# Sends of two per step and two pairs begun per period in a two-layer graph-attention and expert kernel

## Chip, cores and metric

The kernel runs on one core of one Trainium2 chip. The metric is the device time of one execution in microseconds (us), lower is better; the time before is the median of three runs. An engine is named as the profile names it: PE is TensorE's matrix multiply and PEld its weight load, DVE is VectorE, ACT is ScalarE, POOL is GpSimd, SP is SyncE, which issues most of the transfers.

## What is computed

There are 64 graphs ("batches") of 256 nodes with 256 features, and one adjacency matrix. Two layers follow each other. `_layernorm` has no weights.

```
x = x + _L0_gnn_ref(_layernorm(x), adj, L0_gnn_W, L0_gnn_a)      # attention with 4 heads, elu
x = x + _L0_ffn_ref(_layernorm(x), L0_ffn_weight, L0_ffn_bias)   # one linear map
x = x + _L1_gnn_ref(_layernorm(x), adj, L1_gnn_W, L1_gnn_a)      # attention with 1 head, relu
x = x + _L1_ffn_ref(_layernorm(x), L1_ffn_router_w, w1, b1, w2, b2)

# _L1_ffn_ref: 8 experts, each token goes to its best two
logits = tokens @ router_w.T
rw, re = top_k(softmax(logits), 2);  rw = rw / rw.sum(-1)
for e in range(8):
    h = gelu(tokens @ w1[e] + b1[e])
    out = out + combine[:, e:e+1] * (h @ w2[e] + b2[e])          # out starts as tokens
```

The input of the last part is the normed `x`, and it is also added once to the result together with `x`.

## The kernel before

**Tiles.** A batch is two tiles of 128 rows. The first three parts and the router's logits of a batch are done by `batch_layers` (L485). The last part is not computed for all experts: 62 of the 64 batches are routed, that is, every row is written ("sent") to its two experts' regions in an HBM buffer `xs`, and the experts then work through full regions in units of 256 rows, called pairs of tiles. The last two batches are not routed; for them all eight experts are computed densely (`dense_expert`).

**Chunks.** Routed batches are grouped into chunks of 4 (twelve times), 2 (six times) and 1 (twice). A chunk of four batches has 8 tiles. When the logits of a chunk's last batch are there, `route` (L907) does, spread over several steps: the two best experts of every row (`top_two`), the place of every row in its expert's region (the matmuls L924 and L925 and the scan L933), the weights, the sends, and the allotting of pairs (`allot`, in two parts). A send is one indirect DMA issued by POOL (L890): 128 rows of one tile go to the places of their first or second expert, so a tile has two sends and a full chunk sixteen.

**Pairs.** In all there are 131 pairs: 1 for the first chunk, 8 for each of the other full chunks, 4 or 2 for the small ones, and 14 at the end that are not full. `expert_pair` (L710) loads a pair's rows (`xr`, L726, behind all the sends of its chunk), then its expert's weights (`we`), turns the rows on DVE (L116), computes the hidden layer on PE (`hidden`, L784, 8 matmuls) and gelu on ACT, the second product on PE (L799, 8 matmuls), adds the bias on DVE (L809) and multiplies by the row weights on ACT (L777). Then `scatter` (L814) adds the 256 rows into the output by two indirect DMAs with an add, issued by POOL (L820). The same row may be added to by two pairs, so the two DMAs of each pair wait until the two of the pair before have landed: the scatters form one chain.

**The order.** The program order of every engine is written by the loop at the end (L1058). Jobs are generators, and each `yield` ends a job's work in a step and gives its rank in the next one. A batch begins every third step (`TICKS = 3`), so three steps are one period, and the phase is the step's number modulo 3. Batches overlap: in one period, PE runs some part of each of several batches. In this document period n lasts from the first projection matmul (L384) of batch n to that of batch n+1.

- `later(rank, *phases)` lets a job sleep until a step of one of these phases (as long as batches are still beginning).
- Pairs begin in phase 1: each period adds to `credit`, and every credit of 1 begins one waiting pair. From `DRAIN_AT` (step 180) on the credit of a period is 3. From `QUIET` (step 209) on, one pair begins in every step.
- One scatter at most is begun in each step, behind the sends of that step.
- A pair that begins in step s is turned in s+2, goes through L784 in s+4, L799 in s+5 and L777 in s+6, and is scattered from s+7 on.
- The last dense batch is stored (L863) only after all scatters have landed.

Of buffers the steps of the prediction touch: 8 tiles `xng` of rows to be sent, 5 `xr`, 7 `we`, 9 `y` (the results that wait for their scatter).

Of the kernel before, what the change touches and what calls it, by code (L numbers as in the profile page):

```python
# [27 lines left out]
def kernel(  # L28
# [50 lines left out]
    def bank(name, shape):  # L79
        t = psum.tile([P, 2 * D], F32, tag="bank", name=name, bufs=8)  # L80
        n = 1
        for s in shape:
            n *= s
        t = t[:, :n]
        if len(shape) == 2:
            t = t.rearrange("p (a b) -> p a b", a=shape[0])
        elif len(shape) == 3:
            t = t.rearrange("p (a b c) -> p a b c", a=shape[0], b=shape[1])
        return t
# [317 lines left out]
    for i in range(2):  # L407
        t = keep.tile([P, NT, D + 1], F32, tag=f"q1_{i}", name=f"q1_{i}")
# [207 lines left out]
    def chunk_tile(shape, name, c, bufs=2, dt=F32):  # L616
        return keep.tile([P] + shape, dt, tag=name, name=f"{name}_{c}", bufs=bufs)
# [27 lines left out]
    def two_weights(less, second, ed):  # L645

        nc.vector.tensor_scalar(less, ed, 1.0, None, op0=ALU.add)
        nc.vector.reciprocal(less, less)
        nc.vector.tensor_tensor(second, ed, less, ALU.mult)
        nc.vector.tensor_tensor(less, less, second, ALU.subtract)  # L650
# [231 lines left out]
    def begin(job, rank):  # L882
        active.append([rank, len(order), job])
        order.append(job)
# [16 lines left out]
    def later(rank, *phases):  # L901

        yield rank
        while more and order_steps[-1] % TICKS not in phases:
            yield rank

    def route(c, row0, nt, n, last, xng, lg):  # L907

        rt = lambda shape, name, bufs=2, dt=F32: chunk_tile(shape, name, c, bufs, dt)
        vec, tt = nc.vector, nc.vector.tensor_tensor  # L910
        yield -90

        tail = rt([nt, 3], "tail")
        ohs, ed = top_two(c, nt, lg, tail[:, :, 0])
        m = rt([E, nt], "m")
        tt(m.rearrange("p e t -> p t e"), ohs[:, 0], ohs[:, 1], ALU.add)


        spread = nt == NTC
        yield from later(90, *((0,) if spread else (1, 2)))  # L920

        mf = m.rearrange("p e t -> p (e t)")
        pp = bank("pp", [2, E, nt])
        nc.tensor.matmul(pp[:, 0].rearrange("p e t -> p (e t)"), tri, mf, start=True, stop=True)  # L924
        nc.tensor.matmul(pp[:, 1].rearrange("p e t -> p (e t)"), ones, mf, start=True, stop=True)  # L925
        both = rt([2, E, nt], "both")
        vec.tensor_copy(both, pp)
        pre, tot = both[:, 0], both[:, 1]
        nc.scalar.activation(ed, ed, AF.Exp)
        tt(tot[:, :, 0], tot[:, :, 0], rows[0], ALU.add)  # L930
        run = rt([E, nt], "run")
        if nt == NTC:
            vec.tensor_tensor_scan(  # L933
                run.rearrange("p e t -> p (e t)"), scan_mask.rearrange("p e t -> p (e t)"),
                tot.rearrange("p e t -> p (e t)"), 0.0, ALU.mult, ALU.add,
            )
        else:
            for e in range(E):
                vec.tensor_tensor_scan(
                    run[:, e, :], ones[:, :nt], tot[:, e, :], 0.0, ALU.mult, ALU.add  # L940
                )
        rows[0] = run[:, :, nt - 1]
        tt(pre, pre, run, ALU.add)
        if spread:
            yield from later(90, 2)
        tt(
            ohs, ohs, pre.rearrange("p e t -> p t e")[:, None].to_broadcast([P, 2, nt, E]),
            ALU.mult,
        )
        posf = rt([2, nt], "posf")  # L950
        vec.tensor_reduce(posf, ohs, AX.X, ALU.add)
        pos = rt([2, nt], "pos", 4, I32)
        vec.tensor_copy(pos, posf)
        yield from later(90, *((0,) if spread else (1, 2)))
        two_weights(tail[:, :, 1], tail[:, :, 2], ed)
        for i, xe in enumerate(xng):
            vec.tensor_copy(xe[:, :, D + 1 :], tail[:, i * NT : (i + 1) * NT, :])
        parts = allot(c, n, False)
        if n and not spread:
            next(parts)  # L960
            ids, ef = next(parts)
        if last:
            ends_at = rt([E], "ends_at", 2, I32)
            vec.tensor_copy(ends_at, rows[0])
        yield from later(95, 1, 2)
        mark = len(sent)
        for t in range(nt):
            for k in range(2):
                send(xng[t // NT][:, t % NT, :], pos[:, k, t : t + 1])
            if n and spread and t in (1, 3):  # L970
                ids, ef = next(parts) or (None, None)
            if not last:
                yield from later(95, 1, 2)
            elif t % 2:
                yield 95
        needs = sent[mark:]
        if n:
            regs = {}
            waiting.extend(
                lambda j=j: expert_pair(j, n, ids, ef, regs, needs) for j in range(n)  # L980
            )
        if last:
            parts = allot(c + 1, FLUSH, True)
            next(parts)
            ids2, ef2 = next(parts)
            _, ends_sp = nc.values_load_multi_w_load_instructions(
                ends_at[0:1, :], engines=[mybir.EngineType.SP], min_val=0,
                max_val=(E * CAP - 1) * PAIR, skip_runtime_bounds_check_because="rows of a region",
            )
            filled = []  # L990
            for e in range(E):
                d = nc.sync.dma_start(
                    out=xs_d[bass.ds(ends_sp[e], PAIR), :].rearrange("(p t) c -> p t c", t=2),
                    in_=fill,
                )
                tc.declare_no_dep(
                    d.ins, query=SYNC, group="rows", reason="filling rows lie behind an expert's last row"
                )
                tc.add_to_no_dep_group("rows", d.ins)
                filled.append(d.ins.name)  # L1000
                nc.sync.nop()
            yield 95
            regs2 = {}
            waiting.extend(
                lambda j=j: expert_pair(j, FLUSH, ids2, ef2, regs2, filled)
                for j in range(FLUSH)
            )
# [45 lines left out]
    step, more, credit = 2, True, 0.0  # L1053


    DRAIN_AT, QUIET = TICKS * (B - 4), TICKS * B + 17
    SETUP_AT = 3
    with tc.manual_schedule():  # L1058
        while more or active or waiting or dense_jobs or scatters:
            phase = step % TICKS  # L1060
            if phase == 2 and more:
                nxt = next(batches, None)
                more = nxt is not None
                if more:
                    begin(nxt, 25)
            if step >= SETUP_AT and setup:
                begin(setup.pop(0)(), 90)
            if step >= QUIET:
                if waiting and len(scatters) < 3:
                    begin(waiting.pop(0)(), 90)  # L1070
            elif phase == 1:
                credit = min(credit + (2.0 if step < DRAIN_AT else 3.0), 3.0)
                while waiting and credit >= 1.0:
                    credit -= 1.0
                    begin(waiting.pop(0)(), 90)
            if dense_jobs and step % DENSE == 0:
                begin(dense_jobs.pop(0)(), 90)
            if scatters:
                def one():
                    scatter()  # L1080
                    return
                    yield
                begin(one(), 97)
            order_steps.append(step)
            queue = [(a[0], a[1], a) for a in active]
            heapq.heapify(queue)
            while queue:
                *_, entry = heapq.heappop(queue)
                entry[0] = next(entry[2], None)
                if entry[0] is not None and entry[0] < 0:  # L1090
                    entry[0] = -entry[0]
                    heapq.heappush(queue, (entry[0], entry[1], entry))
            if half_done:
                finish_norms(NT)
            active[:] = [a for a in active if a[0] is not None]
            step += 1
# [35 lines left out]
```

## Time and profile before

| | |
|---|---|
| median of three runs | 1650.05 us (1646.56 to 1652.72) |
| profiled execution, its own time | 1651.53 us |
| its span, first to last instruction | 1649.6 us |
| mean granted TensorE clock | 0.955 |
| PE busy | 1476.3 us, 89% of the span |
| DVE busy | 1323.8 us, 80% |
| ACT busy | 831.0 us, 50% |
| POOL busy | 889.4 us, 54% |
| scatters, L820 on POOL | 262, 1.585 us each |
| sends, L890 on POOL | 248, 1.012 us each |
| moved by DMA | 207.37 MB, mean 126 GB/s |

Busy times are sums over one execution, taken by the hardware profiler. The span is cut into stages that differ: about 300 us in which batches run and no pair does, some 900 us of steady periods with eight pairs to four periods, a stretch with three pairs in each period, and the end, in which no batch is left and pairs and scatters run out. A share of the whole span says little about what limits any one of these stages.

### The profile page before, as it was taken

How to read it: one execution, taken by the hardware profiler on the slowest of the kernel's cores; microseconds unless marked ns; L12 is line 12 of the kernel's file. 1: busy time of each engine (PE TensorE's matmuls, PEld its weight loads, DVE VectorE, ACT ScalarE, POOL GpSimd, SP SyncE). 2: the span in 40 equal slices, each digit the busy share in tenths (PEclk: the TensorE clock that was granted, in tenths of full speed). 3: DMA queues.
4: the chain of work that ended last, by engine and by line, in shares of the span. 5: the costliest groups of instructions: out<-in, count | busy, mean ns of one | idle time of the engine just before them, and what ended most of it. 6: DMA issues, size and time to landing. Idle time of an engine off the chain costs nothing.

```text
span 1649.6 us, 30216 instructions
## 1 busy us (share of the span) xinstructions
PE 1476.3 (89%) x8474; PEld 1299.8 (79%) x8474; DVE 1323.8 (80%) x4494; ACT 831.0 (50%) x1832; POOL 889.4 (54%) x853
## 2 busy tenths in 40 slices
PE   5898888999999999999999999999989997599930
PEld 4777777778888888888888888887878886488820
DVE  6888989999898989898989898999988877545510
ACT  0244344445666666565656666655555565343310
POOL 0121343444757575756575757566664677544444
PEclk8999999999999999999999999999999998799965
DMA  4812123254756565656666675756575667887633
GB/s 109 231 44 58 55 71 101 72 140 113 158 132 135 135 146 135 140 138 145 140 127 156 117 170 108 163 117 146 135 140 124 136 127 152 188 178 135 128 38 45
DMA packets 364132, 207.37 MB, mean 126 GB/s; under 512 B 264248, under 2 KB 334912, under 8 KB 363968
## 3 DMA queue, kind: packets, MB, share of 16 engines
q1 hardware_dynamic: 313344, 137.07, 33.7%
q0 software_dynamic: 49632, 67.39, 22.8%
q8 instruction: 70, 1.15, 0.3%
q10 hardware_dynamic: 992, 0.99, 0.2%
q14 instruction: 94, 0.77, 0.2%
HBM read 116.19 MB, written 89.15 MB: 124 GB/s over the span
## 4 chain that ended last, share of the span: by engine, by line
PE 62%; DVE 21%; DMA 5%; POOL 4%; issue 3%; ACT 3%; SPq 1%; DVEq 0%; POOLq 0%; ACTq 0%
PE pv L475 14%; PE ph L784 13%; PE py L799 12%; PE pq L384 5%; PE pq L419 5%; PE pf L529 4%; DVE z L461 3%; PE pt L368 3%; DVE stats L353 3%; DMA out_dram<-y,xt 3%; POOL out_dram L820 2%; PE pl L599 2%; DVE mv L354 2%; ACT xT L374 1%; PE pd L454 1%
## 5 line engine op out<-in xcount | busy, mean ns | idle before, releaser
L820 POOL DMA_INDIRECT out_dram<-y,xt x262 | 415.4, 1585 | 241.1 <-DMA out_dram<-y,xt 87.6
L475 PE MATMUL pv<-q,z 128*128 128x65 f32 (+1 forms) x2560 | 368.5, 299 | 3.7 <-DVE z L461 3.7
L475 PEld LDWEIGHTS pv<-q,z 128*128 128x128 f32 x2560 | 331.5, 194 | 15.5 <-DVE z L461 4.0
L361 POOL TENSOR_SCALAR rstd<-mv 128x4 f32<-128x4 f32 (+1 forms) x132 | 71.0, 538 | 432.2 <-DVE mv L354 337.1
L890 POOL DMA_INDIRECT xs<-xng,pos x248 | 250.9, 1012 | 68.8 <-issue 65.7
L799 PE MATMUL py<-w2s,hT 128*128 (+1 forms) x1176 | 266.1, 379 | 1.3 <-ACT hT L790 1.2
L784 PE MATMUL ph<-sT,we 128*128 128x256 f32 x1048 | 242.8, 385 | 11.8 <-DVE y L809 9.6
L799 PEld LDWEIGHTS py<-w2s,hT 128*128 128x128 f32 x1176 | 219.5, 190 | 30.0 <-ACT hT L790 2.2
L374 ACT COPY xT<-pt 128x512 f32<-128x512 f32 x192 | 113.3, 590 | 232.5 <-PE pt L368 232.4
L784 PEld LDWEIGHTS ph<-sT,we 128*128 128x128 f32 x1048 | 198.9, 194 | 38.5 <-issue 9.9
L461 DVE SCALAR_TENSOR_TENSOR z<-pd,q,mask 128x256 f32<-128x256 f32 x512 | 211.1, 473 | 0.3 <-PE pd L454 0.2
L790 ACT ACTIVATE hT<-ph,we 128x256 f32<-128x256 f32 x294 | 122.5, 472 | 126.2 <-PE ph L784 103.8
L362 POOL TENSOR_TENSOR rstd<-rstd,mhalf 128x4 f32<-128x4 f32 (+1 forms) x132 | 163.0, 1235 | 11.0
L777 ACT ACTIVATE y<-y,w 128x256 f32<-128x256 f32 x262 | 112.6, 501 | 100.1 <-DVE y L809 100.1
L353 DVE BATCH_NORM_STATS2 stats<-x 128x6 f32<-128x256 f32 x384 | 156.3, 407 | 2.2
L384 PE MATMUL pq<-wx,xT 128*128 128x268 f32 x512 | 139.2, 418 | 8.6 <-DVE wt L257 4.2
L419 PE MATMUL pq<-wx,xT 128*128 128x259 f32 x512 | 129.1, 394 | 15.6 <-ACT xT L374 15.6
L809 DVE TENSOR_TENSOR y<-py,b2s 128x512 f32<-128x512 f32 x131 | 85.8, 686 | 68.6 <-PE py L799 48.8
L384 PEld LDWEIGHTS pq<-wx,xT 128*128 128x128 f32 x512 | 101.8, 204 | 30.4 <-issue 6.9
L419 PEld LDWEIGHTS pq<-wx,xT 128*128 128x128 f32 x512 | 91.9, 189 | 42.0 <-ACT xT L374 30.7
L529 PE MATMUL pf<-wfT,xT 128*128 128x256 f32 x512 | 124.1, 386 | 0.0
L551 ACT ACTIVATE rel<-pv,rinv 128x256 f32<-128x256 f32 x128 | 53.9, 474 | 110.6 <-DVE rinv L482 110.5
(152 smaller groups left out, 2256.1 us busy)
## 6 DMA issues: line engine op xcount, KB each, us to landing
we<-wpack SPq DMA_DIRECT2D x139, 288.0 KB
xr<-xs SPq DMA_DIRECT2D x524, 64.0 KB
xblk<-in_x_dram SPq DMA_DIRECT2D x256, 64.0 KB
xin<-in_x_dram SPq DMA_DIRECT2D x64, 256.0 KB
out_dram<-base SPq DMA_DIRECT2D x64, 256.0 KB
out_dram<-y,xt POOLq DMA_INDIRECT x262, 3.9
xs<-xng,pos POOLq DMA_INDIRECT x248, 2.9
xs<-fill SPq DMA_DIRECT2D x9, 260.0 KB
```

The source lines that it names most:

```text
L353: nc.vector.bn_stats(stats[:, t, :], src[:, t, :])
L362: nc.gpsimd.tensor_tensor(rstd[:, :n], rstd[:, :n], mhalf[:, :n], ALU.pow)
L374: nc.scalar.copy(dst, pt)
L384: nc.tensor.matmul(pq.rearrange("p h c -> p (h c)"), xT[:, k, t * P : (t + 1) * P], wx[:, k, :], start=(k == 0), stop=(k == KT - 1),)
L419: nc.tensor.matmul(pq, xT[:, k, t * P : (t + 1) * P], wx1[:, k, :], start=(k == 0), stop=(k == KT - 1),)
L461: nc.vector.scalar_tensor_tensor(z[:, j, :], pd[:, i, :], q[:, j, h, d + 2 : d + 3], mask[:, j, :], op0=ALU.max, op1=ALU.mult,)
L475: nc.tensor.matmul(pv[:, h, :], z[:, j, t * P : (t + 1) * P], q[:, j, h, : d + 1], start=(j == 0), stop=(j == NT - 1),)
L529: nc.tensor.matmul(pf[:, t, :], xT[:, k, t * P : (t + 1) * P], wfT[:, k, :], start=(k == 0), stop=(k == KT - 1),)
L784: nc.tensor.matmul(ph[:, f, :], we[:, k * D + f * P : k * D + (f + 1) * P], xT[:, k, :], start=(k == 0), stop=(k == KT - 1),)
L799: nc.tensor.matmul(py[:, t, :], hT[:, f, t * P : (t + 1) * P], w2s[:, e, f * D : (f + 1) * D].rearrange("p e c -> p (e c)"), start=(f == 0 ...
L820: d = nc.gpsimd.indirect_dma_start(out=out_rows, out_offset=bass.IndirectOffsetOnAxis(ap=xt[:, t, 0:1].bitcast(I32), axis=0), in_=y[:, t, ...
L890: d = nc.gpsimd.indirect_dma_start(out=xs_d[: E * CAP * PAIR, :], out_offset=bass.IndirectOffsetOnAxis(ap=at, axis=0), in_=xe, in_offset=None,
```

## The change

Three lines of the schedule change. A chunk's sends no longer wait for phases 1 and 2: the first tile is sent in the step after the weights, and each further tile in the next step, whichever its phase. The second part of `allot` moves from behind tile 3 to behind tile 4. And the credit of a period in the steady part is capped at 2, where before a period without waiting pairs could leave a credit over, so that the next one began three.

```diff
@@ route
-        yield from later(95, 1, 2)
+        yield 95
         mark = len(sent)
         for t in range(nt):
             for k in range(2):
                 send(xng[t // NT][:, t % NT, :], pos[:, k, t : t + 1])
-            if n and spread and t in (1, 3):
+            if n and spread and t in (1, 4):
                 ids, ef = next(parts) or (None, None)
             if not last:
-                yield from later(95, 1, 2)
+                yield 95
             elif t % 2:
                 yield 95
         needs = sent[mark:]
@@ the loop that writes the order
             elif phase == 1:
-                credit = min(credit + (2.0 if step < DRAIN_AT else 3.0), 3.0)
+                credit = min(credit + 3.0, 2.0 if step < DRAIN_AT else 3.0)
                 while waiting and credit >= 1.0:
                     credit -= 1.0
                     begin(waiting.pop(0)(), 90)
```

## The prediction, made before the changed kernel was run

> **What bounds the kernel now.** I read the page's table of 40 slices first, then busy time by period (stretches cut at the first L384 of each batch), then the timelines of PE and POOL where a period was too long, and the end of POOL's timeline.
>
> ```profile
> PE   5898888999999999999999999999989997599930
> DVE  6888989999898989898989898999988877545510
> PEclk8999999999999999999999999999999998799965
> ```
>
> PE is full from slice 7 to the 33rd or so; before that it has room, and the last two slices have hardly any PE work. The periods, with the columns length, PE, PEld, DVE, ACT, POOL busy, clock, DMA share, GB/s:
>
> ```profile
> 315.40:333.70 18.30, 15.44 (x94) 12.56 (x95) 16.22 (x56) 7.22 (x18) 10.70 (x12) 1.00 0.36 87
> 333.70:351.20 17.50, 16.29 (x94) 13.89 (x94) 15.75 (x57) 7.34 (x18) 7.41 (x10) 0.90 0.43 99
> 437.20:462.40 25.20, 24.96 (x148) 22.31 (x146) 23.50 (x80) 17.76 (x41) 18.42 (x18) 1.00 0.76 171
> 462.40:483.80 21.40, 21.16 (x129) 18.94 (x129) 20.02 (x61) 12.76 (x28) 10.15 (x11) 1.00 0.49 121
> 483.80:505.10 21.30, 21.06 (x127) 18.85 (x126) 19.40 (x71) 12.95 (x29) 13.88 (x14) 1.00 0.57 115
> 505.10:523.60 18.50, 17.88 (x112) 15.79 (x111) 13.68 (x43) 8.43 (x18) 13.09 (x13) 1.00 0.77 150
> 1106.10:1125.50 19.40, 18.19 (x115) 16.18 (x114) 17.92 (x68) 8.67 (x19) 14.40 (x15) 1.00 0.79 159
> 1125.50:1156.80 31.30, 28.50 (x143) 25.09 (x142) 28.13 (x109) 18.35 (x40) 17.87 (x18) 0.89 0.54 132
> 1199.90:1221.70 21.80, 18.52 (x116) 16.30 (x115) 18.14 (x68) 9.87 (x21) 16.48 (x16) 1.00 0.81 172
> 1221.70:1251.60 29.90, 28.52 (x144) 24.87 (x143) 26.59 (x99) 18.32 (x40) 17.79 (x17) 0.89 0.62 126
> ```
>
> The first two rows (periods 18 and 19) have no pair. The next four are one cycle of a full chunk, periods 24 to 27, with 3, 2, 2 and 1 pairs: PE covers all but 0.3 us of the first three, so a pair is paid at its PE time, 25.2 - 21.4 = 3.8 us. (In most cycles the fourth takes 17.9, with PE at 17.6.) The last four rows are periods 55, 56, 59 and 60, with 1, 3, 1 and 3 pairs: there two chunks' routing overlaps, DVE is busy 28.1 us in period 56, and PE waits for it and then loses its clock:
>
> ```profile
> 1127.54 1.00 PE L475 MATMUL pv<-q,z 128*128 128x65 f32 x8
> 1131.11 5.17 PE L475 MATMUL pv<-q,z 128*128 128x65 f32 x24 [2.56 <-DVE z L461]
> ```
>
> The end is another matter. PE's last work ends at 1580.9, and this goes on until 1645:
>
> ```profile
> 1626.89 1.54 POOL L820 DMA_INDIRECT out_dram<-y,xt  x1 [2.98 <-DMA out_dram<-y,xt]
> 1628.74 1.54 POOL L820 DMA_INDIRECT out_dram<-y,xt  x1 [0.30 <-issue]
> 1633.21 1.54 POOL L820 DMA_INDIRECT out_dram<-y,xt  x1 [2.93 <-DMA out_dram<-y,xt]
> ...
> 1645.39 0.39 SPq L863 DMA_DIRECT2D out_dram<-base  x1
> ```
>
> Each pair's first scatter waits for the DMA before it. Alone, ten pairs from 1581.90 to 1639.68 take 57.78 / 9 = 6.42 us each; beside the last PE work, 16 from 1458.29 to 1575.57 take 7.33 each. The chain of scatters, not PE, ends the kernel, and by then it lags the products by 40 to 50 us.
>
> **The Trainium skill.** "DMA: Bandwidth & Descriptors", section "Anatomy of one DMA — SWDGE (gpsimd) path", puts most of a DMA's fixed 2 us on the confirmation that the data landed; here the second scatter is issued in 1.54 us and the next pair starts 4.5 us after its start, so the wait is of that kind. Its "Rules for kernel authors" say that an accumulating DMA must wait for an earlier one to the same bytes: the chain can't be shortened by issuing faster, only by leaving fewer pairs to its end. "TensorE: Matmul & The Clock Gate", "Part 1: The HAM clock gate", has the PE clock halved after an idle window of about 3.4 us; the trace agrees roughly: the clock stands at 0.5 for 6.8 us from 1132.4, after that wait (shorter, 2.56 us), and again from 1228.0. "PSUM — Partial Sum Buffer", "Engine vs sequencer instructions", calls GpSimd's queue strict FIFO: a send delays whatever stands behind it on POOL.
>
> **The change, part by part.** Counted in the written order of the two programs. Before, a full chunk sends two tiles per period: first send in step s, last in s+10, pairs begin in s+15. After: last send in s+7, pairs begin in s+9. So pairs begin two periods earlier, and each of the forty steady periods from 20 to 59 has two instead of 3, 2, 2, 1. Four pairs more are done by period 59. In steps 201 to 203, after the last batch has begun, two pairs pass L784 instead of 3. When batches end (step 209), 17 pairs wait instead of 20, and the program has 235 steps instead of 238. No instruction is added or removed but for registers.
>
> (a) The early pairs. Period 14 gets the first chunk's one pair and goes from 16.4 to the 17.9 of a one-pair period: +1.5. Period 16 loses it, but period 12, with the same routing and no pair, took 21.0 against its 21.2: -0.2. Periods 18 and 19 get two each and become 21.4: +3.1 and +3.9. Sum +8.2.
>
> (b) Even periods. 25.18 + 21.39 + 21.33 + 17.87 = 85.8 becomes 4 x 21.36 = 85.4: -0.33, in nine cycles -3. It needs DVE to keep up in the heavy period, which is also where `top_two` stands: DVE falls there from 23.5 by one pair's 1.75 us (0.69 turn, 0.69 L809, 0.37 weights) to 21.8, against PE's 21.1. Cover: L924 starts 3.0 to 3.9 us after its DVE operand is ready in periods 20 to 52; one L799 group less takes 1.8 of that. And the one-pair period ahead had left DVE late (the first L475 group of period 24 starts 0.4 us after its last z; after two-pair periods 4.3 to 5.5), which now goes. I take no stall; 0.9 us a cycle as the bad end, +9.
>
> (c) Periods 55/56 and 59/60. Against clean periods of the same pairs (17.87 + 25.18 = 43.05) they take 50.7 and 51.7, an excess of 7.7 and 8.7. With two pairs in 55 and in 59, PE gives DVE 3.5 us more ahead of the jam, the 2.56 us wait and the clock loss after it should shrink; the routing's DVE work stays. I take half, -8; ends 0 and -16.
>
> (d) Steps 201 to 203: one pair less at 3.65 of PE, in a stretch where other waits begin (PE stands 9.33 us in front of L924 at 1394.9); -2, ends 0 and -3.7.
>
> (e) The end. Three pairs fewer in the serial chain at 7.33: -22. Ends: 3 x 6.42 = 19, or 4 x 7.33 = 29 if the chain is full already where it is four ahead.
>
> (f) Sends. A send costs POOL 1.0 + 0.3 us, so two in phase 0 put 2.6 us ahead of the next rstd (L361, L362) in the send periods. POOL idled 1.2 to 9.4 us there waiting for DVE; hidden. Between the other rstd's the queue holds four sends and a scatter pair as before. If the cover were gone, `by` (L560) would be late by up to 2.6, with 1.4 to 7.6 us between its product `xng` and the PE transposes. Zero.
>
> (g) Loads behind sends. Steady chunks' first load is issued 28.4 us after the last send ends (1081.0 to 1109.5). Three steps of 7.1 us go: 7.1 left, against a landing of 2.9 (median) to 5.4. SP just clears it. Were it to wait, the input loads for batches two and three ahead queue behind, which have periods to spare, and `xr` itself is wanted two steps (14 us) later. Zero.
>
> The second part of `allot` stays in the same step (tile 3 before, tile 4 after). Sum: 8.2 - 3 - 8 - 2 - 22 = -26.8; 1651.5 - 26.8 = 1624.7 against the profiled execution's own time, which lies 1.5 above the median of the runs: 1623 there.
>
> **Rivals.** *Back to the start*: early pairs cost 10, nothing is relieved in (c) and (d), and the end gives 19: 1651.5 + 10 - 3 - 19 = 1639; with small stalls of half a microsecond per cycle, 1645. For it: DVE is as busy in 56 as PE. Against: that jam follows a one-pair period.
>
> *DVE becomes the bound of the routing period* (slower than before): period 24 and its like stay at 25.2 with two pairs because DVE's 21.8 and the latency of `top_two` fill it, while the light one still grows to 21.4. That is +3.5 in each of ten cycles, without (b) and (c): 1651.5 + 8.2 + 35 - 2 - 22 = 1671. For it: period 12, with routing and no pair, took 21.0 with DVE at 18.9 and L924 waiting 3.3 us for DVE. Against: the 3 us of slack above. It decides from about 2.7 us a cycle, if (c) fails too.
>
> *More than thought*: (c) goes wholly and the chain is four pairs shorter: 1651.5 + 8 - 3 - 16 - 4 - 29 = 1608.
>
> That the change does not do what it says is excluded: the written order shows 16 L784 matmuls in each period.
>
> **Numbers.** Forecast 0.72 (1612 to 1636), more 0.08, back to the start 0.11, slower 0.09. A change of 0.5% (8 us, below 1641.8 or above 1658.3) is what a measurement here can tell. Forecast, more and a little of the third give 0.82 faster; 0.1 the same, 0.08 slower. Range 1608 to 1643, from the larger gain to the middle of the second rival.
>
> **What would show it.** (b): periods 20 to 54 all 21.3 to 21.5 with PE at 21.1; wrong if a period with L924 reads 22 or more. (a): periods 18 and 19 at about 21.4. (c): the wait in front of L475 near period 56 and the half clock after it smaller or gone. (e): fewer scatters after PE's end or the same lag with an earlier end; wrong if scatters' spacing grows. (f), (g): waits of L726 for `xs` and of ACT for rstd no longer than now (32.3 and 83.4 us in all). The forecast fails as a whole if L924 waits for DVE in every chunk.

## Result, and the profile after

| | before | after |
|---|---|---|
| median | 1649.59 us of 4 runs (1646.56 to 1652.72) | 1633.01 us of 4 runs (1630.33 to 1633.96) |
| profiled execution, its own time | 1651.53 us | 1633.96 us |
| its span | 1649.6 us | 1632.2 us |
| mean granted TensorE clock | 0.955 | 0.958 |
| PE busy | 1476.3 us | 1476.4 us |
| DVE busy | 1323.8 us | 1322.6 us |

The changed kernel takes 0.9897 of the time before, with a 95% interval of 0.9875 to 0.9919. It is faster by about 17 us. PE and DVE do the same work as before. This is PE's row of the slices on the page of after, in tenths:

```profile
PE   5898989899999999999999999999999999589960
```

The stretch in which PE is below nine tenths now ends about a slice later, and the last slices hold a little more PE work than before. The slices are too coarse for a change of 1%, so I cut both traces at the first L384 of some batches, and at the last end of PE. The first cut is at period 5. Where the number of pairs is equal in both kernels, the row says so.

| stretch | before | after | difference |
|---|---|---|---|
| start to period 5 (no pairs) | 87.9 | 88.9 | +1.0 |
| periods 5 to 19 (1 pair before, 5 after) | 263.4 | 277.3 | +13.9 |
| periods 20 to 23 (8 pairs in both) | 86.0 | 85.8 | -0.2 |
| periods 24 to 55 (64 in both) | 688.3 | 686.6 | -1.7 |
| periods 56 to 59 (8 in both) | 96.2 | 96.2 | 0.0 |
| periods 60 to 62 (9 in both) | 79.9 | 76.0 | -3.9 |
| period 63 to PE's last end (41 pairs before, 37 after) | 279.4 | 267.9 | -11.5 |
| PE's last end to the end of the span | 68.7 | 53.6 | -15.1 |

The sum is -17.5, which is the -17.4 of the spans but for rounding. The early stretch pays, the end earns, and the long steady stretch between them stays as it was.

**The early stretch.** Here are periods 14 to 19 as one window, first of before and then of after. The columns are length; busy time of PE, PEld, DVE, ACT and POOL with the number of instructions; PE clock, DMA share and GB/s.

```profile
244.20:351.20 107.00, 96.05 (x584) 82.12 (x584) 98.12 (x338) 48.09 (x115) 47.70 (x57) 0.97 0.32 86
```

```profile
245.30:366.20 120.90, 109.68 (x648) 95.45 (x649) 108.52 (x374) 61.95 (x142) 53.03 (x61) 0.96 0.38 100
```

Four pairs more cost 13.63 us of PE. The time in which PE is idle was 10.95 us (107.00 - 96.05) and is 11.22 us now: taken together nothing of it was used, and the stretch grew by about the pairs' PE time. DVE is busy for about nine tenths of it in both. Its busy time grew by 10.4 us (108.52 - 98.12) and its idle time by 3.5, so the pairs cost more than the DVE work that came with them. Of the two periods that got two pairs each, the second went as forecast and the first did not:

```profile
320.20:344.90 24.70, 22.83 (x127) 20.20 (x128) 23.36 (x85) 16.57 (x37) 7.38 (x9) 0.93 0.39 100
344.90:366.20 21.30, 21.06 (x127) 18.84 (x126) 18.99 (x61) 11.94 (x26) 12.59 (x14) 1.00 0.53 135
```

In period 18 DVE is busy for 23.36 of 24.70 us. The clock is 0.93 in that period and 1.00 in the next, where before it was 1.00 and 0.90; together the two periods took 35.9 us before and take 46.0 now. PE's timeline in period 18 shows the longest wait there:

```profile
337.48 2.89 PE L419 MATMUL pq<-wx,xT 128*128 128x259 f32 x8 [1.87 <-DVE by L563]
```

Period 16 gave up its pair and still grew by 1.2 us. Before, the pair's products covered most of PE's wait for the routing (L924); now PE waits all of it, and the clock stands at half for 6.8 us from 300.9 (before, for 3.4 us in this period, from 279.1). First before, then after:

```profile
298.84 0.43 PE L924 MATMUL pp<-m,tri 128*128 128x64 f32 x2 [0.94 <-DVE m L916]
```

```profile
302.19 0.66 PE L924 MATMUL pp<-m,tri 128*128 128x64 f32 x2 [3.33 <-DVE m L916]
```

**Steady periods.** One cycle of after, periods 24 to 27, all with two pairs:

```profile
452.00:473.70 21.70, 21.46 (x132) 19.24 (x130) 19.23 (x64) 13.34 (x30) 16.04 (x16) 1.00 0.69 151
473.70:495.10 21.40, 21.16 (x129) 18.94 (x129) 19.82 (x62) 12.81 (x29) 11.05 (x11) 1.00 0.61 121
495.10:516.40 21.30, 21.06 (x127) 18.85 (x126) 19.11 (x70) 12.94 (x29) 12.66 (x13) 1.00 0.61 135
516.40:537.70 21.30, 21.06 (x127) 18.85 (x126) 18.72 (x60) 13.06 (x29) 15.94 (x17) 1.00 0.69 153
```

In every row PE is busy for all but 0.24 us. The four together take 85.7 as the rounded rows add up. Cut more finely, the cycles from period 28 to 51 take 85.77 on average in both kernels. Uneven periods of 25.2 and 17.9 lost nothing against even ones, since PE was full in both.

**The jam.** Periods 55, 56, 59 and 60 of after:

```profile
1116.80:1138.60 21.80, 21.56 (x132) 19.28 (x131) 19.76 (x77) 11.19 (x26) 14.71 (x16) 1.00 0.63 144
1138.60:1165.10 26.50, 24.94 (x128) 22.02 (x127) 25.09 (x92) 15.51 (x34) 16.02 (x18) 0.87 0.49 104
...
1213.00:1234.70 21.70, 21.46 (x131) 19.32 (x130) 19.60 (x80) 11.96 (x27) 13.02 (x12) 1.00 0.73 134
1234.70:1260.70 26.00, 24.80 (x143) 21.83 (x142) 24.76 (x87) 16.80 (x37) 15.94 (x15) 1.00 0.59 136
```

and PE's timeline in period 56:

```profile
1140.58 1.00 PE L475 MATMUL pv<-q,z 128*128 128x65 f32 x8
1142.91 5.28 PE L475 MATMUL pv<-q,z 128*128 128x65 f32 x24 [1.33 <-DVE z L461]
```

The wait for `z` is half as long as before (1.33 against 2.56), but the clock still falls: period 56 has 0.87, period 60 now has 1.00. Period 56, with one pair fewer than before, lost 4.8 us of its 31.3; periods 57 and 58, with as many as before, grew by 4.9 together (21.7 and 21.3 to 24.1 and 23.9). So the four periods from 56, with eight pairs in both kernels, take the same 96.2.

**The end.** POOL's last scatters and the last store:

```profile
1615.91 1.54 POOL L820 DMA_INDIRECT out_dram<-y,xt  x1 [3.07 <-DMA out_dram<-y,xt]
1617.76 1.54 POOL L820 DMA_INDIRECT out_dram<-y,xt  x1 [0.30 <-issue]
1622.30 1.54 POOL L820 DMA_INDIRECT out_dram<-y,xt  x1 [3.00 <-DMA out_dram<-y,xt]
...
1627.94 0.41 SPq L863 DMA_DIRECT2D out_dram<-base  x1
```

The first scatters of the last two pairs start 1622.30 - 1615.91 = 6.39 us apart, like the 6.42 of before. The chain still ends the kernel, 53.6 us behind the last PE work. From period 63 to the end it is 26.6 us shorter with four pairs fewer: 6.65 each. Counted in links, 46 pairs begin their scatter behind that cut before and 42 after.

### The profile page after: what moved, and what is told of

Read it like the earlier page. It is cut to its first block, busy times and chain, and to the rows that moved or that the text cites. A ratio compares the mean times of both kernels' runs of the same rounds, so it can differ in the third digit from the quotient of the medians.

```text
span 1632.2 us, 30214 instructions
## 1 busy us (share of the span) xinstructions
PE 1476.4 (90%) x8474; PEld 1300.9 (80%) x8474; DVE 1322.6 (81%) x4494; ACT 831.6 (51%) x1836; POOL 888.9 (54%) x853
## 4 chain that ended last, share of the span: by engine, by line
PE 63%; DVE 22%; DMA 4%; POOL 3%; issue 3%; ACT 3%; SPq 1%; DVEq 0%; POOLq 0%; ACTq 0%
PE pv L475 15%; PE ph L784 13%; PE py L799 13%; PE pq L384 6%; PE pq L419 5%; PE pf L529 4%; DVE z L461 4%; PE pt L368 3%; DVE stats L353 3%; PE pl L599 2%; POOL out_dram L820 2%; DMA out_dram<-y,xt 2%; DVE mv L354 2%; ACT xT L374 1%; PE pd L454 1%
## 5 line engine op out<-in xcount | busy, mean ns | idle before, releaser
L475 PE MATMUL pv<-q,z 128*128 128x65 f32 (+1 forms) x2560 | 366.9, 299 | 1.3 <-DVE z L461 1.3
L475 PEld LDWEIGHTS pv<-q,z 128*128 128x128 f32 x2560 | 330.6, 194 | 12.8 <-DVE z L461 1.5
L361 POOL TENSOR_SCALAR rstd<-mv 128x4 f32<-128x4 f32 (+1 forms) x132 | 59.4, 450 | 459.9 <-DVE mv L354 368.7
L784 PE MATMUL ph<-sT,we 128*128 128x256 f32 x1048 | 244.1, 386 | 9.5 <-DMA we<-wpack 7.3
L784 PEld LDWEIGHTS ph<-sT,we 128*128 128x128 f32 x1048 | 199.5, 194 | 36.9 <-issue 7.7
L384 PE MATMUL pq<-wx,xT 128*128 128x268 f32 x512 | 138.5, 417 | 8.1 <-DVE wt L257 4.2
L384 PEld LDWEIGHTS pq<-wx,xT 128*128 128x128 f32 x512 | 101.7, 203 | 29.3 <-issue 6.9
L354 DVE BATCH_NORM_AGGREGATE mv<-stats 128x2 f32<-128x6 f32 x512 | 93.1, 182 | 17.5
```

The costliest lines, as they stand in the source:

```text
L384: nc.tensor.matmul(pq.rearrange("p h c -> p (h c)"), xT[:, k, t * P : (t + 1) * P], wx[:, k, :], start=(k == 0), stop=(k == KT - 1),)
L475: nc.tensor.matmul(pv[:, h, :], z[:, j, t * P : (t + 1) * P], q[:, j, h, : d + 1], start=(j == 0), stop=(j == NT - 1),)
L784: nc.tensor.matmul(ph[:, f, :], we[:, k * D + f * P : k * D + (f + 1) * P], xT[:, k, :], start=(k == 0), stop=(k == KT - 1),)
```

## Experiments

The theory at this point: the change moves four pairs from the end, where each costs a link of the scatter chain, to an early stretch, where each costs its PE time; the even credit by itself gains little. The rivals: the gain comes from the even credit and the smaller jam; the sends' new place costs or gains something by itself; or the loads' new waits on SP take part of the gain. Edits are shown against the changed kernel unless another is named.

### The sends alone

```diff
-                credit = min(credit + 3.0, 2.0 if step < DRAIN_AT else 3.0)
+                credit = min(credit + (2.0 if step < DRAIN_AT else 3.0), 3.0)
```

> The sends of the changed kernel with the credit of the kernel before: pairs begin two periods earlier, in the pattern 3, 2, 2, 1, and 17 pairs are left when the batches end. Theory A (the gain is the three pairs that leave the serial chain of scatters at the end, and even periods are worth little): about 1635 to 1639, that is two thirds or more of the gain, with the jam at period 56 back (31 us instead of 26.5). Theory B (the even periods carry the gain): 1643 to 1650. Theory A also expects the first cycle of pairs to cost as much early as in the changed kernel, 10 us or more up to period 22.

Measured: 1634.57 us (1630.48 to 1635.62), 0.9905 [0.9883, 0.9928]. It keeps nearly the whole gain. It has one early pair more (six before period 20) and pays +14.9 for them. From period 63 to the end it takes 315.4 us against 348.1, with five pairs fewer: 6.5 each. Its periods 56 to 59 are worse than before, 101.6 against 96.2, and not in the way expected: period 56 takes 23.5 us, and the time is lost in 57 and 58 (28.6 and 27.8).

### The credit alone

```diff
-        yield 95
+        yield from later(95, 1, 2)
...
-            if n and spread and t in (1, 4):
+            if n and spread and t in (1, 3):
...
-                yield 95
+                yield from later(95, 1, 2)
```

> The credit of the changed kernel with the sends of the kernel before: two pairs in every steady period, but begun when they were before, and 20 pairs left at the end. Theory A: 1643 to 1648, only the jam near periods 56 and 60 relieved by about 5 us, nothing in periods 24 to 54, and the end as before. Theory B: 1633 to 1640.

Measured: 1641.55 us (1637.25 to 1649.62, 19 runs), 0.9964 [0.9949, 0.9979]. A gain of 6 us is there, which lies between the two expectations. The early stretch and the number of pairs behind period 63 are those of before (263.4 us, 41 pairs). Its place is the jam: periods 56 to 59 take 93.2 and 60 to 62 take 76.8, against 96.2 and 79.9; periods 28 to 51 take 85.77 per cycle here too. So the rival holds in part: the even credit is worth a third of the gain when it stands alone. On top of the early sends no gain from it can be told (0.9905 without it, 0.9897 with it, and the intervals overlap).

### The sends early, the pairs held back

```diff
+        for _ in range({8: 4, 4: 3}.get(nt, 0)):
+            yield 95
         needs = sent[mark:]
```

with the old credit; what is left of the change is where the sends stand on POOL.

> The sends of the changed kernel, but the pairs held back until they began before, and the old credit: the same work in the same steps as before, but for the steps of the sends. If the place of the sends on POOL's queue costs nothing (step f of the prediction): 1647 to 1652, no change. If sends in phase 0 delay the rstd behind them: 1655 or more. SP's waits for the sends should be back at about 30 us from the 175 us of the changed kernel.

Measured: 1653.28 us (1647.77 to 1659.49, 22 runs), 1.0027 [1.0014, 1.0039]. So without the early pairs there is no gain at all, and a loss of about 4 us. What costs these 4 us stays open. All 131 pairs stand where they stood before in PE's order, and in the one profile of this kernel, 1.2 us longer than that of before, period 63 begins 2.2 us earlier and PE's last work ends 1.8 us earlier; it falls behind only in the chain of scatters after that (71.7 us against 68.7). One part of it was plainly not as expected. SP's waits, with total, number and longest, in before and here:

```profile
SPq L726 <- DMA xs<-xng,pos: 32.3, 7, 12.4
```

```profile
SPq L726 <- DMA xs<-xng,pos: 230.2, 39, 13.7
```

The loads stand as far behind their own sends as before and wait far more.

### Half of the shift

```diff
+        for _ in range({8: 1}.get(nt, 0)):
+            yield 95
         needs = sent[mark:]
```

A full chunk's pairs become ready one step later, which is one period later for their beginning.

> The changed kernel with the pairs of the full chunks begun one period later: 18 pairs are left when the batches end instead of 17 (20 before), and no loads stand close behind their sends. If a pair less at the end is worth about 7 us and the early pairs cost about 3.5 us each as measured, one pair goes back to the end (+7 to +9) and two fewer run early (-7): 1631 to 1637, about as fast as the changed kernel. If SP's 175 us of waiting for sends hurts the changed kernel: clearly faster than it, below 1630. If each period of earlier begin is worth half of the gain: 1640 to 1643.

Measured: 1638.89 us (1638.15 to 1642.07), 0.9946 [0.9927, 0.9965]. Three pairs run before period 20, and 39 are left behind period 63, halfway between the two kernels. The early stretch pays +5.1, the part behind period 63 earns 348.1 - 336.6 = 11.5, or 5.8 per pair. The time lies about halfway too, above the 1631 to 1637 expected, where one pair and not two was counted as going back to the end.

### Three pairs less in the chain

```diff
         y, xt = scatters.pop(0)
+        if len(added) >= 2 * (PAIRS - 3):
+            return
...
-        while b == B - 1 and (scatters or len(added) < 2 * PAIRS):
+        while b == B - 1 and (scatters or len(added) < 2 * (PAIRS - 3)):
```

> The changed kernel without the scatters of the last three of the 131 pairs: their rows are not added to the output, all else is computed. Theory A (the end is the serial chain of scatters): the end moves forward by 3 x 6.4 = 19 us against the changed kernel, to about 1614, and PE's last work does not move. Rival (PE or the last products end the kernel, and the scatters' lag would be made up): less than 8 us, 1625 or more.

Measured: 1615.22 us (1613.82 to 1618.8), 0.9787 [0.9768, 0.9806]. Its span is 1612.9, 19.3 less than that of after (19.8 when both are counted from period 5). The last PE work is not earlier: 270.6 us behind the start of period 63, against 267.9. All the gain is behind it. Its last scatters:

```profile
1596.35 1.54 POOL L822 DMA_INDIRECT out_dram<-y,xt  x1 [3.11 <-DMA out_dram<-y,xt]
...
1602.80 1.54 POOL L822 DMA_INDIRECT out_dram<-y,xt  x1 [3.06 <-DMA out_dram<-y,xt]
```

They keep their spacing, 1602.80 - 1596.35 = 6.45 us. Each link that is taken away is worth 19.8 / 3 = 6.6 us of the whole time: the chain of scatters sets the end, shown by taking part of it away.

### Less DVE work

```diff
-        x1b = work.tile([P, NT, D], F32, tag="x1b", name="x1b", bufs=1)
-        nc.vector.tensor_add(x1b, x1, bias_f[:, None, :].to_broadcast([P, NT, D]))
...
-                x2[:, t, :], pf[:, t, :], rstd[:, t : t + 1], x1b[:, t, :],
+                x2[:, t, :], pf[:, t, :], rstd[:, t : t + 1], x1[:, t, :],
```

> The changed kernel without the addition of the second part's bias on DVE (L521, 0.69 us for each batch); the product's line then adds the rows without the bias. If the stretch up to period 20 is bound by DVE: its periods from 5 to 20 shrink by 0.3 to 0.7 us each, 5 to 11 us by period 20, and the periods from 24 to 54 do not move (PE-bound, less than 1 us in all), and the jam from 55 to 59 loses 1 to 4 us: about 1620 to 1627. If PE bounds the early stretch: less than 2 us by period 20.

This kernel leaves out the bias of the second part. Measured: 1614.85 us (1610.36 to 1617.05), 0.9773 [0.9751, 0.9796], a larger gain than expected. The addition takes 0.691 us per batch, so the fifteen periods 5 to 19 lose 10.4 us of DVE work. They got 14.2 us shorter (277.3 to 263.1), with the same pairs. In the steady periods 24 to 54 the same saving brought nothing: 664.8 us in both. The windows of period 18 and of period 24 of this kernel:

```profile
306.60:328.50 21.90, 21.01 (x128) 18.86 (x127) 20.81 (x77) 14.70 (x34) 7.38 (x9) 1.00 0.44 113
...
435.60:457.30 21.70, 21.46 (x131) 19.22 (x131) 18.59 (x63) 13.33 (x30) 16.11 (x16) 1.00 0.70 151
```

Period 18 is 2.8 us shorter than in after and PE's clock is whole there; period 24 is as long as in after. So in the early stretch DVE's chain of work sets the pace, and in the steady stretch PE does. Whether it is the sum of DVE's work or the time that the addition adds to a batch's own chain is not separated by this run. That the early stretch gave 14.2 for 10.4 of work I did not follow further; the better clock of period 18 is part of it.

### Four sends in a step

```diff
-            if n and spread and t in (1, 4):
+            if n and spread and t in (1, 3):
                 ids, ef = next(parts) or (None, None)
-            if not last:
-                yield 95
-            elif t % 2:
+            if t % 2:
                 yield 95
```

A full chunk is sent in four steps instead of eight, so its pairs begin one period earlier still.

> The changed kernel with two tiles, four sends, in each step: the pairs of the full chunks begin one period earlier still, 15 pairs are left when the batches end. By the exchange measured so far (a pair that leaves the end gives 6.6 us, one that runs early costs 3.5): two more early pairs +7, two fewer at the end -13: 1626 to 1630. If POOL can't take 5.2 us of sends and a scatter pair in a step of 7.1 us: rstd comes late, periods with sends grow by 1 us or more, 1640 or more.

Measured: 1627.58 us (1624.93 to 1629.25), 0.9854 [0.9836, 0.9872]. Seven pairs run before period 20, for +19.3; 35 are left behind period 63. From there to the end it takes 31.3 us less than before, 5.2 for each of six pairs. That the time falls into the range expected (1626 to 1630) is luck, as the reason given for it did not hold. Against after, the two further pairs cost 5.4 us early (282.7 against 277.3) and the end earns only 4.7 (316.8 against 321.5): 41 pairs begin their scatter behind period 63, one fewer than in after, so the chain lost one link and not two. This trade doesn't pay any more. In the profiles, what makes this kernel faster than after is the jam, where periods 56 to 59 take 89.5 us against 96.2; no run shows why.

### Loads that wait for their own sends only

A load of `xr` reads rows whose place is known only at run time, so in the kernel it waits for every send that stands ahead of it in program order, those of the next chunk too. Here it names the sends of its own chunk (the rest of the edit keeps a list of the sends and puts empty instructions on SP beside the loads):

```diff
         for load in loads:
+            keep_these = [sent_ins[name] for name in needs]
+            tc.declare_no_dep(
+                load.ins, query=SYNC, group="rows", keep=keep_these,
+                reason="rows sent by a later chunk lie in other pairs",
+            )
```

> The changed kernel, but a pair's loads no longer wait for the sends of the chunk behind theirs (the waits of SP's program for POOL's transfers go from 97 to 68). SP's waits for sends should fall from 175 us to 60 or less. If they were hidden: 1631 to 1635, no change. If they cost what the held sends lost (3 to 4 us) or the weights that come late at the end (7.3 us): 1625 to 1630.

SP's waits in after and in this kernel:

```profile
SPq L726 <- DMA xs<-xng,pos: 175.5, 32, 13.6
```

```profile
SPq L728 <- DMA xs<-xng,pos: 8.6, 3, 3.7
```

The waits are gone. Measured: 1631.19 us (1627.61 to 1638.6), 0.9893 [0.9866, 0.9920], against 0.9897 [0.9875, 0.9919] for after. The two can't be told apart: 167 us of waiting on SP cost nothing that these runs resolve. The one profile, of the fastest of the four runs, is 5.8 us shorter behind period 63 (315.7 against 321.5) with as many scatters, and equal ahead of it; so a cost of a few us at the end is neither shown nor excluded.

### Both together, and the addition on POOL

Four sends in a step with loads that wait for their own sends:

> Four sends in each step together with loads that wait for their own chunk's sends only. The first gave 1627.6. If SP's waits are hidden everywhere but at the end: 1622 to 1628, the difference to four sends alone within 5 us and all of it after period 63. If the two parts share the same gain: 1626 to 1630.

Measured: 1625.17 us (1623.56 to 1628.8), 0.9850 [0.9828, 0.9872], against 0.9854 [0.9836, 0.9872] for four sends alone: not to be told apart either. This profile, too, is shorter behind period 63, by 4.3 us.

The same, and in the first twenty batches the addition of `x1b` on POOL instead of DVE:

```diff
-        nc.vector.tensor_add(x1b, x1, bias_f[:, None, :].to_broadcast([P, NT, D]))
+        adder = nc.gpsimd if b < 20 else nc.vector
+        adder.tensor_add(x1b, x1, bias_f[:, None, :].to_broadcast([P, NT, D]))
```

> The kernel with four sends and loads behind their own sends, and the bias addition (L521) of the first 20 batches on POOL instead of DVE; nothing is left out. If DVE bounds the stretch up to period 20 and POOL (3 to 13 us busy in those periods) has room: 6 to 14 us gained there, and nothing elsewhere: about 1612 to 1620. If the longer addition on POOL delays the rstd behind it or DVE's own work: no gain or a loss up to period 20, 1625 or more.

Measured: 1622.67 us (1620.37 to 1625.73), 0.9836 [0.9814, 0.9858]. It has the lowest median of all kernels that compute the whole, about 27 us below before and 10 below after. Its interval overlaps with that of the kernel without the addition on POOL, and its early stretch isn't shorter (284.5 against 283.7 us), so the share of the addition in this isn't shown. The 6 to 14 us expected of it did not come.

The addition on POOL in the changed kernel alone:

> The changed kernel with the bias addition of the first 20 batches on POOL. As the run without the addition gained 14 us up to period 20 and this one does the work elsewhere: 5 to 12 us by period 20 if DVE's time alone mattered there, 1621 to 1628, and periods 24 to 54 as in the changed kernel. A loss up to period 20 means that POOL or the handing over costs more than DVE's 0.69 us each.

Measured: 1634.35 us (1630.05 to 1635.37), 0.9906 [0.9884, 0.9927]: no gain against after. Periods 5 to 9, in which no chunk is being sent, take 81.3 us instead of 84.4; periods 10 to 19 take 197.0 instead of 192.9, and period 16 alone 25.4 instead of 22.4. POOL's timeline and DVE's in that period:

```profile
295.33 0.98 POOL L891 DMA_INDIRECT xs<-xng,pos  x1 [0.30 <-issue]
296.34 1.27 POOL L522 TENSOR_TENSOR x1b<-x,bias_f 128x512 f32<-128x512 f32 x1
```

```profile
295.78 1.92 DVE L632 TENSOR_TENSOR eq<-eq,em 128x64 f32<-128x64 f32 x1
```

The addition stands in POOL's queue between sends and takes 1.27 us there instead of 0.69 on DVE. The Trainium skill's "GPSIMD Engine Reference", section "3.1 Elementwise — side-by-side cycle accounting", has such an addition 1.96 times as long on GpSimd as on VectorE at 2048 elements; here, at 512, it is 1.27 / 0.69 = 1.84 times. Nor does DVE gain the time: its instruction beside the addition, which takes 0.22 us in after (median), lasts 1.92 us here, until POOL's addition is done. From 181.8 us on, nine of the eleven additions go with a DVE instruction stretched to 1.7 to 2.0 us; over all twenty additions DVE's instructions beside them take 19.5 us longer than their medians in after, and the additions taken from DVE are worth 13.8.

### The ledger of the runs

Times in us of each profile; pairs whose first product (L784) runs before period 20 and behind period 63, and links: pairs that begin their scatter behind period 63.

| kernel | pairs early | periods 5-19 | periods 24-62 | pairs late | links late | period 63 to end | ratio to before |
|---|---|---|---|---|---|---|---|
| before | 1 | 263.4 | 864.3 | 41 | 46 | 348.1 | 1 |
| after | 5 | 277.3 | 858.7 | 37 | 42 | 321.5 | 0.9897 |
| sends alone | 6 | 278.3 | 865.3 | 36 | 41 | 315.4 | 0.9905 |
| credit alone | 1 | 263.4 | 856.6 | 41 | 46 | 346.2 | 0.9964 |
| sends early, pairs held | 1 | 261.8 | 863.8 | 41 | 46 | 351.4 | 1.0027 |
| half of the shift | 3 | 268.5 | 857.8 | 39 | 44 | 336.6 | 0.9946 |
| four sends in a step | 7 | 282.7 | 853.2 | 35 | 41 | 316.8 | 0.9854 |
| own waits alone | 5 | 277.2 | 859.0 | 37 | 42 | 315.7 | 0.9893 |
| four sends, own waits | 7 | 283.7 | 853.2 | 35 | 41 | 312.5 | 0.9850 |

The columns of the early pairs and the late links carry the explanation: each pair that moves costs 2.6 to 3.5 us early (half of the shift: 5.1 / 2 = 2.6; sends alone: 14.9 / 5 = 3.0; four sends: 19.3 / 6 = 3.2; after: 13.9 / 4 = 3.5), and each link that leaves the end earns 5.8 to 6.65 (half of the shift: 11.5 / 2; four sends: 31.3 / 5 = 6.3; sends alone: 32.7 / 5 = 6.5; after: 26.6 / 4). Kernels of this table with the same number of links differ by up to 5.8 us there, so a single profile fixes this price only roughly.

## Why the prediction was right, and where not

The forecast was 1623 us, 1612 to 1636 for this outcome and 1608 to 1643 over all; measured were 1633.01. That lies inside, but nearer to the rival *Back to the start* (1639, which is 1638 as a median) than to 1623. The mechanism was right: the change moves pairs away from the end, where the chain of scatters counts each of them, and the runs with three links less, with half of the shift and with the sends alone show that. The sum of the parts was -26.8 and came to -17.4. The terms one by one, by its letters:

- **(a) early pairs, +8.2 forecast, +13.9 measured: mis-sized.** The term set two pairs at the length of a steady two-pair period, 21.4, as if PE's 2.9 and 1.2 us of idle time in periods 18 and 19 were room. Period 19 did become 21.3, but period 18 became 24.7, period 14 took 2.9 more where 1.5 was forecast, and period 16 grew by 1.2 though it lost its pair; periods 15 and 17 changed by -1.5 and +1.1, which the sum had at nothing. Of PE's 10.95 us of idle time in periods 14 to 19 before, 8.5 were waits for DVE, which was as busy as PE there, and pairs bring DVE work too. The run with less DVE work shows that the stretch yields to DVE and the steady stretch doesn't. The rows in the windows of before said as much: in period 18 DVE was busy for 16.22 of 18.30 us and PE for 15.44, so DVE led; in period 19, where the forecast held, PE led with 16.29 to 15.75. How the 13.9 us divide between DVE's work, the uncovered wait in period 16 and the clock is not shown.
- **(b) even periods, -3 forecast; (c) the jam, -8 forecast; both together -5.6 measured (periods 24 to 62): over-sized.** A cycle of four steady periods takes 85.77 in both, so (b) is nil: the 85.8 of its own sum and the 85.4 beside it differed only by taking 21.36 for a period with L924, which takes 21.7. The 1.7 us of periods 24 to 55 fell in the first cycle (0.6) and the last (1.1). Of (c), the wait before L475 went from 2.56 to 1.33 us and the loss of clock in period 60 went away (-3.9), but in period 56 it stayed, and the time gained there was lost in periods 57 and 58. The credit alone does better in this place (93.2 us for periods 56 to 59), the sends alone worse (101.6), so the two halves of the change pull in opposite directions there. By what path two sends in every step cost time in the jam wasn't tried; the loads' waits are not it (96.1 with them taken away).
- **(d) and (e) together, -24 forecast, -26.6 measured: right.** Four pairs fewer behind period 63, at 6.65, where the text took one fewer before the end of the batches and three fewer in the chain at 7.33.
- **(f) the sends' place, 0 forecast: open.** ACT's waits for rstd fell from 83.4 to 51.9 us, as the text asked, but that goes with the even credit: they are 56.2 with the credit alone, 80.8 with the sends alone and 91.6 with the pairs held back. That last run lost about 4 us, and its profile doesn't tell whether POOL's queue or the loads' waits cost them.
- **(g) loads behind sends, 0 forecast: not contradicted, but the first reason was wrong.** The text counted the time from the last send of a load's own chunk. SP's waits, which were to be no longer than 32.3 us, went to 175.5, because the load waits for every send ahead of it in the program, and with sends in every phase the next chunk's sends stand just ahead of it. POOL's sends and SP's load in after:

```profile
518.18 1.10 POOL L890 DMA_INDIRECT xs<-xng,pos  x1 [0.20 <-issue]
519.58 0.98 POOL L890 DMA_INDIRECT xs<-xng,pos  x1 [0.30 <-issue]
```

```profile
522.10 1.99 SPq L726 DMA_DIRECT2D xr<-xs  x4
```

The load starts 2.5 us after the start of the send before it, which is one of the next chunk that it doesn't need. The second ground given, that what queues behind it has periods to spare, is the one that held: the run with loads that wait for their own sends took these waits away and moved the time by nothing that can be resolved.
- **The start** is 1.0 us later in after. Kernels whose early code is the same lie between 87.6 and 91.7 us there, so this is no effect of the change.

Of the rivals, *DVE becomes the bound of the routing period* fell: every period from 20 to 54 took 21.3 to 21.7, and L924 started 2.83 us after its DVE operand was ready (some 2 was forecast). *Back to the start* came nearest in (a), where 13.9 exceeded even its 10, and it was right that the jam would be relieved little; its 19 at the end was too little. *More than thought* was right about four links and wrong about the jam.

## What to carry over

Before work is moved into a stage because one engine has idle time there, look at who ends that idle time: where another engine is as busy, the idle time may be no room at all, as in this kernel, where 13.6 us of PE time cost 13.9. A serial chain at the end of a kernel is shortened by starting its links earlier, and its price per link (5.8 to 6.65 us here) can be set against the price of the early place (2.6 to 3.5 here) before the change is made. Count the links that really leave the end, not the products that move: with four sends in a step two more pairs passed PE early, and the end lost one link more. To see what a transfer waits for, count all that stands ahead of it in program order on the same buffer, not only what it needs.

## What was not expected of the hardware

- **The clock fell after a wait still shorter than the one of before.** The Trainium skill's "TensorE: Matmul & The Clock Gate", section "Part 1: The HAM clock gate", gives an idle window of about 3.4 us. In after PE waits 1.33 us before L475 at 1142.91, and the clock stands at half for 6.8 us from 1144.0; before, it was a wait of 2.56 us with the same 6.8. The timeline shows no single wait as long as that window there. Halving the wait did not save the clock in period 56; in period 60 it stayed whole.
- **Long waits of SP cost nothing that could be measured.** SP waited 175.5 us for sends in after and 8.6 us in the run with own waits, and the medians lie 1.8 us apart with intervals that overlap. A few us at the end are not excluded.
- **The links of the scatter chain keep their length.** 6.39 us alone in after, 6.45 with three fewer, 6.42 in before, of which twice 1.54 are the work of POOL for the two DMAs and about 3 the wait until the second has landed. No run made a link shorter; the gains at the end came from links begun earlier or left out.
- **An addition moved from DVE to POOL still took DVE's time.** In the changed kernel with the addition on POOL, a DVE instruction beside it lasted 1.92 us instead of 0.22, up to the end of POOL's addition. No run shows the cause.
